# A last block of at most 64 keys with both parts of its weights on the partitions: layer 1's attention output in two passes instead of three

## The chip, the cores and the metric

The kernel runs on one core of one Trainium2 chip. The metric is the device time of one execution in microseconds. Before the change three runs took 1855.35, 1860.09 and 1863.01 us; their median, 1860.09 us, is the time before.

## What is computed

Two layers act on x (2 x 1024 x 512). Each adds an attention and a feed-forward part, both of the normalised x, to x. The change is in layer 1's attention, which has 32 heads of 128, in groups of four that share one of 8 key/value heads:

```python
scores = jnp.einsum('bhqd,bhkd->bhqk', q, k) * scale
scores = jnp.where(causal, scores, -1e9)
attn = jax.nn.softmax(scores, axis=-1)
out = jnp.einsum('bhqk,bhkd->bhqd', attn, v)
...
return out @ Wo.T
```

Inputs and outputs are float32. Layer 0 does a single-head attention without a mask beside a mixing of four streams with Sinkhorn normalisation; layer 1's feed-forward part is a dense product with routed low-rank terms.

## The kernel before

**Numbers in two parts.** Every float32 operand of a product is split into a float16 high part and a float16 low part, the rest. A product takes three matmuls (`PASSES`, line 81: high with high, high with low, low with high), added up in PSUM. `mm3` (line 88) issues them for all products but the attention output, which has its own loop, `attn_out` (line 345).

**Rows of layer 1.** `layer1_attn` walks 16 groups (2 batches x 8 key/value heads), each in 32 steps. A step s is one "row": 32 queries of each of the four heads, 128 partitions in all, against the first W = 32(s+1) keys, as the causal mask allows. Four steps make a block of 128 queries: c = s // 4 is the block, r = s % 4 the row in it. Rows r = 0 and 1 form half k = 0, rows 2 and 3 half k = 1. So the number of keys in the last block of 128 is 32, 64, 96 and 128 for r = 0 to 3; half k = 0 never has more than 64 of them. Constants named below: P = 128, S = 1024, LB = 3 buffers of `Phl`, XB = 4 of `xr`.

**One row.** `row_step` issues the scores of a row (tile `s` in PSUM), then the second part of the row before:

1. DVE (L283, L287) scales, masks and takes the row minimum into `P`; ACT takes the exponential and its sum (L291).
2. `rows_hi`: DVE takes the reciprocal (L302), ACT scales it (L303) and writes the weights' high part into `Phl` (L308).
3. `rows_lo`: DVE writes the low part into `Phl` in one instruction (L314); in layer 0 some rows use POOL (L312). If W is no multiple of 128, POOL fills the rest of both parts with zeros (L319), queued behind a DVE instruction. Then SP issues one DMA transpose (L320) of the row's 2m blocks of 128, m = ceil(W/128), high blocks first, low blocks after, into `PT`: keys on the partitions, queries along the row.

**Output.** `group_av` sums, for one half of block c, V's transposed blocks times `PT` into 256 columns of the PSUM tile `av`: c+1 blocks of keys, three matmuls each, 128 rows deep. After half 1, ACT and DVE turn `av` into two float16 parts `ao` (L104, L105) for the product with Wo (L88, result added to `acc` at L737).

**What sets the order.** `layer1_attn` writes out the order of work by hand: `at(g, s, f)` puts a piece of filling work after row step s of group g. Half k of block c's output stands at step 4c + 2k + 5, its product with Wo at 4c + 10; the next group's keys and values, its queries, and its weights stand in between; so do, in the first eight groups, layer 0's remaining mixing of batch 1, the gating and the feed-forward part (`put`, `extra`). V of a group (tile `V`, [128, part, block, 128]) is written during the group before. The Tile framework turns this into an order for each engine and allots buffers: a tile of a tag waits until one of the tag's buffers is free. The tag `xr` is used by the loads of batch 1's mixing (L607), for the gating's hidden values (L1063) and by eight normalised tiles for the gating in the seventh group (L1008).

**Queues.** SP issues all transposes and the loads of x; POOL issues the loads of weights; each engine works through its own instructions in order.

**The only matmuls with fewer rows.** Layer 0's output adds its bias with matmuls one row deep, `row` (1 x 128) times `bo` (1 x 512), at L484; the three matmuls of the product with Wo follow at L486.

Of the kernel before, what the change touches and what calls it, by code (L numbers as in the profile page):

```python
# [9 lines left out]
F16 = mybir.dt.float16  # L10
F32 = mybir.dt.float32
AF = mybir.ActivationFunctionType
ALU = mybir.AluOpType
# [3 lines left out]
P = 128  # L17
S = 1024
NB = 2
NT = S // P  # L20
# [8 lines left out]
FB, PB, LB, XB, WB = 4, 3, 3, 4, 9  # L29
QR = 32  # L30
# [21 lines left out]
def tile_model(ctx: ExitStack, tc: tile.TileContext, out: bass.AP, a: dict):  # L52


    nc = tc.nc
    V, A, G = nc.vector, nc.scalar, nc.gpsimd
# [7 lines left out]
    def T(tag, shape, dt=F32, bufs=None):  # L64
        count[0] += 1
        kw = {} if bufs is None else {"bufs": bufs}
        return sb.tile(shape, dt, tag=tag, name=f"{tag}_{count[0]}", **kw)
# [13 lines left out]
    PASSES = ((0, 0), (0, 1), (1, 0))  # L81
# [21 lines left out]
    def evac(src, hl_hi, hl_lo, scale):  # L103
        A.activation(hl_hi, src, AF.Copy, scale=scale)  # L104
        return V.scalar_tensor_tensor(hl_lo, src, scale, hl_hi, ALU.mult, ALU.subtract)  # L105
# [77 lines left out]
    last_hi, last_lo, last_low = [None], [None], [None]  # L183
# [8 lines left out]
    def behind(i, j, wait=False):  # L192

        kind = mybir.DependencyClass.Sync if wait else mybir.DependencyClass.NoSync
        tc.add_manual_dep(i.ins, j.ins.name, mybir.DependencyInfo(
            kind, mybir.DependencyReason.DATA), reason="behind")
# [69 lines left out]
    def share(got, n, k, make):  # L266

        if k % n == 0:
            got[0] = make()
        return got[0][:, k % n]  # L270

    P_of, hl_of = [None], [None]
# [21 lines left out]

    def rows_parts(W, n, k):

        m = -(-W // P)
        hl = share(hl_of, n, k, lambda: T("Phl", [P, n, 2 * S // n], F16, bufs=LB))
        return hl[:, :2 * m * P].rearrange("p (l k) -> p l k", l=2)

    def rows_hi(Pm, r, W, pool, hl):
        V.reciprocal(r[:, 1:2], r[:, 0:1])  # L302
        A.activation(r[:, 1:2], r[:, 1:2], AF.Copy, scale=PSCALE)  # L303
        if pool:
            A.activation(Pm[:, :W], Pm[:, :W], AF.Copy, scale=r[:, 1:2])
            A.activation(hl[:, 0, :W], Pm[:, :W], AF.Copy)
        else:
            A.activation(hl[:, 0, :W], Pm[:, :W], AF.Copy, scale=r[:, 1:2])  # L308

    def rows_lo(Pm, r, W, pool, hl, dst):  # L310
        if pool:
            G.tensor_tensor(hl[:, 1, :W], Pm[:, :W], hl[:, 0, :W], ALU.subtract)  # L312
        else:
            lo = V.scalar_tensor_tensor(hl[:, 1, :W], Pm[:, :W], r[:, 1:2], hl[:, 0, :W],  # L314
                                        ALU.mult, ALU.subtract)
            last_low[0] = lo
        if W < hl.shape[2]:

            behind(G.memset(hl[:, :, W:], 0.0), lo)  # L319
        nc.sync.dma_start_transpose(dst, hl.rearrange("p l k -> p (l k)"))  # L320

    pending = []

# [14 lines left out]
        count[0] += 1  # L338
        return ps.tile([P, 512], F32, tag="av", name=f"av_{count[0]}", bufs=BV)

    def attn_out(p, Vh, PT, nj):

        for j in range(nj):
            for k, (l, r) in enumerate(PASSES):
                nc.tensor.matmul(p, Vh(j, l), PT(r * nj + j),  # L345
                                 start=(j == 0 and k == 0),
                                 stop=(j == nj - 1 and k == 2))


    SC0 = 1.0 / (math.sqrt(128.0) * 1024.0)  # L350
# [331 lines left out]
    def fetch(src):  # L682
        st = T("f2k", [P, 512], bufs=FB)
        nc.gpsimd.dma_start(st, src)
        return st
# [42 lines left out]
    def qproj(b, w, Q, hh, half):  # L728

        p = proj_T(lambda c, l: w[:, l, c, :], xT1[b], half)  # L730
        evac(p.rearrange("p (b q) -> p b q", q=QR), Q[:, 0, :, hh, :], Q[:, 1, :, hh, :], 0.125)
# [6 lines left out]
        if last:  # L738
            nc.scalar.dma_start(out[(b * NT + t) * P:(b * NT + t + 1) * P, :], acc[b, t])

    def group_av(Vh, PT, c, k, p):


        attn_out(p.rearrange("p (h b q) -> p b h q", h=4, q=QR)[:, 2 * k:2 * k + 2].rearrange(
                     "p b h q -> p h b q"), lambda j, l: Vh[:, l, j, :],
                 lambda n: PT[:, n].rearrange("p b (h q) -> p h b q", q=QR), c + 1)
        if k == 0:
            return None
        ao = T("ao", [P, 2, 4, P], F16, bufs=2)
        hi, lo = [ao[:, l].rearrange("p h q -> p (h q)") for l in range(2)]  # L750
        evac(p, hi, lo, 1.0 / PSCALE)
        return ao
# [3 lines left out]
    def fetch_q(g, hh):  # L756
        qw[g, hh] = fetch(a["Wq"][4 * (g % NG) + hh])
# [8 lines left out]
    def layer1_attn(kv0, start, extra):  # L766


        N, NS = NB * NG, S // QR
        fill = {}  # L770

        def at(g, s, f):
            g, s = g + s // NS, s % NS
            fill.setdefault((g, s), []).append(f)

        kvs, Qs, PTs, avs, aos, wos = [{} for _ in range(6)]

        def q_unit(g, u):
            half, hh = divmod(u, 4)
            if hh == 0:  # L780
                Qs[g, half] = T("Q", [P, 2, NS // 2, 4, QR], F16, bufs=2)
            qproj(g // NG, qw[g, hh], Qs[g, half], hh, half)

        def fetch_wo(g, hh):
            n = 4 * (g % NG) + hh
            wos[g, hh] = fetch(a["WoT"][n * P:(n + 1) * P, :])

        def split_wo(g, hh):
            wos[g, hh] = parts_of(wos[g, hh], "wo", 32.0, WB)

        def av(g, c, k):
            if k == 0:
                avs[g, c] = out_tile()
            aos[g, c] = group_av(kvs[g]["V"], PTs[g, 2 * c + k], c, k, avs[g, c])

        def wo(g, c):
            wo_block(g // NG, c, aos[g, c], [wos[g, h] for h in range(4)], g % NG == NG - 1)

        kvs[0], fs = kv0
        start(fs[2:], lambda u: q_unit(0, u))  # L800
        for hh in range(4):
            fetch_wo(0, hh)
            split_wo(0, hh)
        for g in range(N):
            if g + 1 < N:
                new = (g + 1) % NG == 0
                kvs[g + 1], fs = kv((g + 1) // NG, (g + 1) % NG)
                at(g, KVN - 2 if new else 1, fs[0])
                for k, f in enumerate(fs[1:]):
                    at(g, KVN + 2 * k if new else 1 + 4 * k + 2 * (k == 0), f)  # L810
                for hh in range(4):
                    at(g, 5 + 4 * hh, lambda g=g, hh=hh: fetch_q(g + 1, hh))
                    at(g, 7 + 4 * hh, lambda g=g, hh=hh: split_q(g + 1, hh))
                for u in range(4):
                    at(g, QNN + 2 * u if new else QN + 4 * u, lambda g=g, u=u: q_unit(g + 1, u))
                for hh in range(4):
                    s = 26 + 2 * hh if new else 22 + 3 * hh
                    at(g, s - 2, lambda g=g, hh=hh: fetch_wo(g + 1, hh))
                    at(g, s, lambda g=g, hh=hh: split_wo(g + 1, hh))
            for u in range(4):  # L820
                at(g, QH + (1 if (g + 1) % NG == 0 else 3) * u, lambda g=g, u=u: q_unit(g, 4 + u))
            for c in range(NT):
                for k in range(2):
                    at(g, 4 * c + 2 * k + AVD, lambda g=g, c=c, k=k: av(g, c, k))
                at(g, 4 * c + WOD, lambda g=g, c=c: wo(g, c))
        for k, fs in extra.items():
            fill[k] = fs + fill.get(k, [])
        for g in range(N + 1):
            for s in range(NS):
                if g < N:  # L830
                    c, r = divmod(s, NR)

                    n = 4 if c < 2 else 2 if c < 4 else 1
                    if c < 4 and r == 0:
                        PT = T("PT", [P, 2 * (c + 1), NR, P], F16, bufs=3)
                        for k in range(2):
                            PTs[g, 2 * c + k] = PT[:, :, 2 * k:2 * k + 2]
                    elif c >= 4 and r % 2 == 0:
                        PTs[g, s // 2] = T("PT", [P, 2 * (c + 1), 2, P], F16, bufs=3)
                    Qt, q0 = Qs[g, s // (NS // 2)], s % (NS // 2)  # L840
                    row_step(lambda l: Qt[:, l, q0].rearrange("p h q -> p (h q)"),
                             kvs[g]["K"], QR * (s + 1), True, SC1, PTs[g, s // 2][:, :, r % 2], False, n, r)
                elif pending:
                    row_step()
                for f in fill.pop((g, s), []):
                    f()
        assert not fill, sorted(fill)
# [131 lines left out]
    PTs = attn0_rows(0, 0, *f0[0][:2], lambda: adv(CA))  # L979
    ys0 = branch0(0, *f0[0][3:5], lambda: adv(CB))  # L980
    attn0_out(0, 0, f0[0][2], PTs)
    PTs = attn0_rows(0, 1, *f0[0][:2], lambda: adv(CA))
# [6 lines left out]
    for half in range(2):  # L989
# [5 lines left out]
        PTs = attn0_rows(1, half, *f0[1][:2], lambda: adv(CD))  # L995
# [153 lines left out]
```

## Time and profile before

| what | value |
|---|---|
| median of the runs | 1860.09 us |
| the profiled execution | 1855.46 us |
| its span, first to last instruction | 1853.7 us |
| mean granted TensorE clock | 0.976 of full |
| TensorE busy | 1715.7 us |
| VectorE (DVE) busy | 1447.6 us |
| ScalarE (ACT) busy | 1194.1 us |
| GpSimd (POOL) busy | 910.6 us |
| DMA transposes `PT<-Phl` | 528, of them 512 in layer 1 |
| matmuls of the attention output (L345) | 3648, of them 3456 in layer 1 |

The profile is of one execution. PE is TensorE's matmuls, PEld its weight loads, which can run beside a matmul. A group of instructions is given as line, engine, operation, out<-in by the program's names, shapes, count, then busy time and the mean length of one in ns, then the engine's idle time just before them with what ended it. Matmuls overlap, so the mean length of one is longer than the distance between two. In a timeline a row is a run of like instructions: its start, its length, and in brackets the idle time before it. "issue" stands for time in which an engine waited for nothing that the profile shows.

### The profile page before, as it was taken

The page shows a single profiled execution, that of the slowest core. Times are in us where ns is not written, and L with a number is a line of the kernel's source. Part 1 is how long each engine was busy: PE and PEld are TensorE (multiplying, and loading weights), DVE is VectorE, ACT ScalarE, POOL GpSimd, SP SyncE. Part 2 cuts the span into 40 slices and gives each one's busy share as a digit, 9 for nine tenths or more (in the row PEclk, how much of TensorE's full clock was granted, in tenths as well). Part 3 has the DMA queues.
Part 4 walks back from the last instruction along what each step waited for, and adds up shares of the span by engine and source line. Part 5 has one row for each costly group of instructions (what it writes and reads, how often), then busy time and mean ns, then how long its engine had stood idle before and what let it go on. Part 6 is the DMA issues. An engine that isn't in the chain of part 4 may idle for free. (4 is left out here: it accounts for less than half of the span.)

```text
span 1853.7 us, 35094 instructions
## 1 busy us (share of the span) xinstructions
PE 1715.7 (93%) x11458; PEld 1046.0 (56%) x11458; DVE 1447.6 (78%) x4050; ACT 1194.1 (64%) x2917; POOL 910.6 (49%) x1540
## 2 busy tenths in 40 slices
PE   4756399999999999998999999999999999999998
PEld 3434146566666556655555556666666666656565
DVE  8888978988888877777976867777777777777675
ACT  3848665656676778776544756666666767676554
POOL 5567639768775455647634333424242433335200
PEclk9878699999999999999999999999999999999999
DMA  7435225666574657468546555656565656566455
GB/s 211 82 56 124 67 51 131 143 115 144 113 147 102 143 115 158 111 131 158 137 92 141 130 120 126 146 111 150 107 151 115 142 117 140 117 141 139 101 123 120
DMA packets 707306, 230.26 MB, mean 124 GB/s; under 512 B 689953, under 2 KB 690081, under 8 KB 707122
## 3 DMA queue, kind: packets, MB, share of 16 engines
q1 hardware_dynamic: 691666, 180.75, 47.2%
q0 software_dynamic: 13152, 43.07, 8.5%
q10 hardware_dynamic: 2304, 4.20, 0.7%
q8 instruction: 90, 1.47, 0.4%
q14 instruction: 94, 0.77, 0.1%
HBM read 52.81 MB, written 4.19 MB: 31 GB/s over the span
## 5 line engine op out<-in xcount | busy, mean ns | idle before, releaser
L291 ACT ACTIVATE P<-P,nm 128x1024 f32<-128x1024 f32 (+31 forms) x528 | 391.3, 742 | 250.0 <-DVE nm L283 234.8
L314 DVE SCALAR_TENSOR_TENSOR Phl<-P,r,Phl 128x1024 f16<-128x1024 f32 (+31 forms) x515 | 434.4, 853 | 85.9 <-ACT Phl L308 79.5
L88 PE MATMUL s<-K,Q 128*128 128x512 f16 (+22 forms) x2400 | 440.7, 317 | 19.5 <-DVE P L287 11.6
L345 PE MATMUL av<-PT,V 128*128 128x256 f16 x3648 | 447.7, 274 | 7.5 <-DMA PT<-Phl 6.8
L345 PEld LDWEIGHTS <-V 128*128 128x128 f16 x3648 | 357.0, 98 | 94.7 <-DMA PT<-Phl 8.3
L308 ACT ACTIVATE Phl<-P,r 128x1024 f16<-128x1024 f32 (+31 forms) x515 | 370.0, 731 | 22.3 <-DMA PT<-Phl 3.3
L88 PE MATMUL pp<-xT,wq 128*128 128x512 f16 x1536 | 372.9, 381 | 6.3 <-DVE acc L737 3.2
L88 PE MATMUL pp<-wo,ao 128*128 128x512 f16 x1536 | 369.9, 379 | 2.9 <-ACT ao L104 2.7
L94 POOL TENSOR_SCALAR f2k<-f2k 128x512 f32<-128x512 f32 x164 | 109.5, 668 | 499.9 <-DVE Phl L314 444.5
L88 PEld LDWEIGHTS <-Q 128*128 128x128 f16 x2400 | 223.2, 98 | 178.2 <-issue 28.4
L88 PEld LDWEIGHTS <-wq 128*128 128x128 f16 x1536 | 149.6, 98 | 173.8 <-issue 8.5
L88 PEld LDWEIGHTS <-ao 128*128 128x128 f16 x1536 | 149.4, 98 | 156.5 <-ACT ao L104 4.8
L287 DVE TENSOR_SCALAR_CACHE_REDUCE P<-s 128x512 f32<-128x512 f32 (+15 forms) x272 | 152.6, 562 | 21.7 <-PE s L88 19.7
L283 DVE CUSTOM_DVE_ANT_0 P<-s,mask,nm 128x272 f32<-128x272 f32 (+15 forms) x256 | 157.3, 615 | 8.7 <-PE s L88 1.0
L303 ACT ACTIVATE r<-r 128x1 f32<-128x1 f32 x528 | 96.2, 193 | 66.2 <-DVE r L302 65.4
L319 POOL MEMSET Phl<- 128x192 f16 (+2 forms) x384 | 72.6, 209 | 133.5 <-DMA PT<-Phl 95.7
L302 DVE RECIPROCAL r<-r 128x1 f32<-128x1 f32 x528 | 79.2, 155 | 75.3 <-ACT P L291 72.1
L104 ACT ACTIVATE ao<-av 128x512 f16<-128x512 f32 x128 | 75.1, 587 | 92.2 <-PE av L345 92.0
L283 DVE CUSTOM_DVE_ANT_0 P<-s,mask 128x32 f32<-128x32 f32 (+15 forms) x256 | 104.3, 432 | 27.6 <-PE s L88 27.1
L104 ACT ACTIVATE Q<-pp 128x512 f16<-128x512 f32 x128 | 74.5, 582 | 76.7 <-PE pp L88 72.2
L737 DVE SCALAR_TENSOR_TENSOR acc<-pp,acc 128x512 f32<-128x512 f32 x128 | 87.4, 682 | 41.0 <-PE pp L88 40.6
L105 DVE SCALAR_TENSOR_TENSOR Q<-pp,Q 128x512 f16<-128x512 f32 x128 | 87.6, 684 | 34.9 <-ACT Q L104 34.6
(254 smaller groups left out, 2119.1 us busy)
## 6 DMA issues: line engine op xcount, KB each, us to landing
f2k<-in_Wq POOLq DMA_DIRECT2D x64, 256.0 KB, 3.2
f2k<-in_WoT POOLq DMA_DIRECT2D x64, 256.0 KB, 3.3
PT<-Phl SPq DMA_TRANSPOSE x528, 3.2
acc<-in_x SPq DMA_DIRECT2D x16, 256.0 KB, 4.6
f2k<-in_Wup POOLq DMA_DIRECT2D x16, 256.0 KB, 3.5
out<-acc ACTq DMA_DIRECT2D x16, 256.0 KB, 3.5
xr<-in_x SPq DMA_DIRECT2D x12, 256.0 KB, 4.1
f2k<-in_Wlat POOLq DMA_DIRECT2D x8, 256.0 KB, 5.5
```

The lines of the kernel that those rows point to most:

```text
L88: nc.tensor.matmul(dst, lhs(l), rhs(r), start=(i == 0 and j == 0), stop=(i == n - 1 and j == 2))
L94: first = G.tensor_scalar(stage, stage, scale, 1.0, ALU.mult, ALU.mult)
L104: A.activation(hl_hi, src, AF.Copy, scale=scale)
L105: return V.scalar_tensor_tensor(hl_lo, src, scale, hl_hi, ALU.mult, ALU.subtract)
L283: last_row[0] = V.tensor_tensor_reduce(Pm[:, o:o + w], pt[:, :w], mask[:, 512 - w:], -scale, first, ALU.add, ALU.min, nm[:, k:k + 1])
L287: last_row[0] = V.tensor_scalar(Pm[:, o:o + w], pt[:, :w], -scale, first, ALU.mult, ALU.min, accum_out=nm[:, k:k + 1])
L291: A.activation(Pm[:, :W], Pm[:, :W], AF.Exp, bias=last, scale=-1.0, accum_out=r[:, 0:1])
L303: A.activation(r[:, 1:2], r[:, 1:2], AF.Copy, scale=PSCALE)
L308: A.activation(hl[:, 0, :W], Pm[:, :W], AF.Copy, scale=r[:, 1:2])
L314: lo = V.scalar_tensor_tensor(hl[:, 1, :W], Pm[:, :W], r[:, 1:2], hl[:, 0, :W], ALU.mult, ALU.subtract)
L345: nc.tensor.matmul(p, Vh(j, l), PT(r * nj + j), start=(j == 0 and k == 0), stop=(j == nj - 1 and k == 2))
L737: V.scalar_tensor_tensor(acc[b, t], p, 1.0 / 256.0, acc[b, t], ALU.mult, ALU.add)
```

## The change

For rows with 1 to 64 keys in the last block (32 and 64, so half k = 0), that block of `Phl` is laid out anew: its first 64 columns hold the high part, the other 64 the low part of the same keys. The row then has 2c+1 blocks: c high ones, the mixed one, c low ones. The transpose puts the mixed block's two parts on partitions 0 to 63 and 64 to 127.

The output's last block then takes two matmuls: V's high part, standing twice on the partitions, times the whole mixed block (128 rows), and V's low part times the high weights (partitions 0 to 63, 64 rows). The doubled V is a tile `Vm` of tag `xr`, filled once in a group by two SBUF-to-SBUF copies of 64 partitions on SP's queue, placed at step 2. DVE writes the low part of such a row in two pieces where c > 0. The zero fill covers what is left of each 64: two times 32 columns for W % 128 = 32, nothing for 64. Rows with 96 or 128 keys in the last block, and all of layer 0, stay as they are.

```diff
     def rows_parts(W, n, k):
+        c, w = divmod(W, P)
+        hl = share(hl_of, n, k, lambda: T("Phl", [P, n, 2 * S // n], F16, bufs=LB))
+        if 0 < w <= 64:
+            hl = hl[:, :(2 * c + 1) * P]
+            o = c * P
+            lo = [(o, W, hl[:, o + 64:o + 64 + w])]
+            if c:
+                lo.insert(0, (0, o, hl[:, o + P:]))
+            pad = hl[:, o:o + P].rearrange("p (l k) -> p l k", l=2)[:, :, w:] if w < 64 else None
+            return hl, hl[:, :W], lo, pad
         m = -(-W // P)
-        hl = share(hl_of, n, k, lambda: T("Phl", [P, n, 2 * S // n], F16, bufs=LB))
-        return hl[:, :2 * m * P].rearrange("p (l k) -> p l k", l=2)
+        hl = hl[:, :2 * m * P]
+        v = hl.rearrange("p (l k) -> p l k", l=2)
+        return hl, v[:, 0, :W], [(0, W, v[:, 1, :W])], v[:, :, W:] if W < m * P else None
...
     def rows_lo(Pm, r, W, pool, hl, dst):
-        if pool:
-            G.tensor_tensor(hl[:, 1, :W], Pm[:, :W], hl[:, 0, :W], ALU.subtract)
-        else:
-            lo = V.scalar_tensor_tensor(hl[:, 1, :W], Pm[:, :W], r[:, 1:2], hl[:, 0, :W],
-                                        ALU.mult, ALU.subtract)
-            last_low[0] = lo
-        if W < hl.shape[2]:
-
-            behind(G.memset(hl[:, :, W:], 0.0), lo)
-        nc.sync.dma_start_transpose(dst, hl.rearrange("p l k -> p (l k)"))
+        whole, hi, los, pad = hl
+        for a0, a1, lo in los:
+            if pool:
+                G.tensor_tensor(lo, Pm[:, a0:a1], hi[:, a0:a1], ALU.subtract)
+            else:
+                last_low[0] = V.scalar_tensor_tensor(lo, Pm[:, a0:a1], r[:, 1:2], hi[:, a0:a1],
+                                                     ALU.mult, ALU.subtract)
+        if pad is not None:
+
+            behind(G.memset(pad, 0.0), last_low[0])
+        nc.sync.dma_start_transpose(dst[:, :whole.shape[1] // P], whole)
...
-    def attn_out(p, Vh, PT, nj):
-
-        for j in range(nj):
-            for k, (l, r) in enumerate(PASSES):
-                nc.tensor.matmul(p, Vh(j, l), PT(r * nj + j),
-                                 start=(j == 0 and k == 0),
-                                 stop=(j == nj - 1 and k == 2))
+    def attn_out(p, Vh, PT, nj, mixed=None):
+        full = nj - (mixed is not None)
+        todo = [(Vh(j, l), PT(r * nj + j)) for j in range(full) for l, r in PASSES]
+        if mixed is not None:
+            todo += [(mixed, PT(full)), (Vh(full, 1)[:64], PT(full)[:64])]
+        for k, (v, pt) in enumerate(todo):
+            nc.tensor.matmul(p, v, pt, start=(k == 0), stop=(k == len(todo) - 1))
...
-                 lambda n: PT[:, n].rearrange("p b (h q) -> p h b q", q=QR), c + 1)
+                 lambda n: PT[:, n].rearrange("p b (h q) -> p h b q", q=QR), c + 1,
+                 None if k else Vm[:, c])
...
+        def twice(g):
+            Vm = kvs[g]["Vm"] = T("xr", [P, NT, P], F16, bufs=XB)
+            for k in range(2):
+                nc.sync.dma_start(Vm[64 * k:64 * k + 64], kvs[g]["V"][0:64, 0])
...
+            at(g, 2, lambda g=g: twice(g))
```

## The prediction

> **What bounds the kernel now.** I read the page's busy times first, then busy time in two stretches of layer 1, then the instruction groups by shape, then the chain of waits inside one group, then the timeline around the only matmuls with few rows.
>
> The page's part 1, each engine's busy time:
>
> ```profile
> PE 1715.7 (93%) x11458; PEld 1046.0 (56%) x11458; DVE 1447.6 (78%) x4050; ACT 1194.1 (64%) x2917; POOL 910.6 (49%) x1540
> ```
>
> A busy TensorE need not be a full one, so I look at stages. Layer 1's rows begin at 262 us (first score matmul of 32 columns) and its sixteen groups take some 92 us each; the later groups start at 1086. Busy time in two stretches (columns: PE, PEld, DVE, ACT, POOL, granted clock, DMA share, GB/s):
>
> ```profile
> 262.00:1086.00 824.00, 796.30 (x5384) 485.75 (x5382) 667.60 (x1837) 544.49 (x1376) 499.09 (x889) 0.99 0.59 129
> 1086.00:1800.00 714.00, 713.79 (x4768) 442.21 (x4766) 528.76 (x1460) 467.09 (x1139) 250.82 (x460) 1.00 0.59 127
> ```
>
> In the second stretch TensorE never rests; in the first it rests 27.7 us of 824 and DVE is 81% busy. Whether it runs at its own pace shows in the chain of one group (1178 to 1270), which is TensorE alone:
>
> ```profile
> 1182.20 2.62 PE av L345 x24
> 1184.82 4.53 PE pp L88 x21
> ```
>
> 2.62/24 is 0.109 us for a matmul of 256 columns, 4.53/21 is 0.216 us for one of 512: time follows the columns. So TensorE sets layer 1's time, and every matmul added or taken away counts nearly in full.
>
> **The change: passes taken away.** The attention-output group:
>
> ```profile
> L345 PE MATMUL av<-PT,V 128*128 128x256 f16 x3648 | 447.7, 274 | 7.5 <-DMA PT<-Phl 6.8 <-DVE ao L105 0.6
> ```
>
> 3456 of the 3648 are layer 1's (16 groups x 2 halves x 3 x 36 blocks). The half k=0 (rows 0 and 1 of each four, 32 and 64 keys in the last block) takes two passes for that block instead of three: one matmul less in each of 16 x 8 = 128 sums. The chain's pace values them at 128 x 0.109 = -14.0 us; the group's busy share (447.7/3648 = 0.123) would give -15.7, but holds the ends of runs. I take -14.0. Their weight loads are hidden.
>
> **The change: a matmul of 64 rows.** Of the two passes left, one reads 128 rows (both weight parts against V doubled), the other only 64. Every other layer-1 matmul has 128 rows. No 64-row matmul stands in the trace; the nearest row is layer 0's bias (L484), one row deep among 128-row matmuls. TensorE timeline at 91 us, then the weight loads there (start, length, in brackets the idle time before):
>
> ```profile
> 91.09 0.71 PE L345 MATMUL av<-PT,V 128*128 128x256 f16 x5
> 91.73 0.60 PE L484 MATMUL pp<-wo,row 1*128 1x512 f16 x2
> 92.27 0.82 PE L486 MATMUL pp<-wo,wo 128*128 128x512 f16 x3
> 93.02 1.03 PE L484 MATMUL pp<-wo,row 1*128 1x512 f16 x4
> ```
>
> ```profile
> 91.09 0.42 PEld L345 LDWEIGHTS <-V 128*128 128x128 f16 x4
> 91.73 0.11 PEld L484 LDWEIGHTS <-row 1*128 1x128 f16 x2 [0.21 <-issue]
> 92.26 0.33 PEld L486 LDWEIGHTS <-wo 128*128 128x128 f16 x3 [0.42 <-issue]
> 93.02 0.33 PEld L484 LDWEIGHTS <-row 1*128 1x128 f16 x3 [0.42 <-issue]
> ```
>
> Five av matmuls from 91.09 should free the array at 91.09 + 5 x 0.109 = 91.635; the one-row matmul starts at 91.73, 0.095 late. Two of 512 columns from there end at 92.162; the 128-row one starts at 92.27, 0.108 late. Three more end at 92.918; the next one-row matmul starts at 93.02, 0.102 late. Inside a run of equal rows nothing is lost. The second view shows how: within a run the next weights load while a matmul runs, at a change of row count they load only after it, with an idle gap put down to no releaser. A change costs about 0.10 us, in either direction.
>
> The 64-row matmul comes last in its sum: 128 rows before it, 128 rows after it, so two changes each, 128 x 2 x 0.10 = +25.6 us. Bounds: 0 if 64 rows need no change of the array, 0.11 if each costs the worst seen (+28.2); below nothing is excluded, as the matmul streams the same 256 columns.
>
> Two rules of the Trainium skill bear on this. "TensorE: Matmul & The Clock Gate", section "Why this matters for your kernels", says a single matmul of 32 rows takes as long as one of 128: by that alone the sum stays -14.0. "TensorEngine Tiling (Array Packing)", section "Key Properties", speaks against the change: going to another tiling mode drains the engine, and its "Tiling Modes" gives 64 rows a mode of their own. It states no price; if I estimate a drain as the 128 cycles that the first page gives for the array's depth, at its 2.4 GHz, that is 0.053 us, 128 x 2 x 0.053 = +13.7, and the sum is about nothing. The row has 0.10 for the same kind of change, so I take +25.6, net **+11.7 us** on TensorE.
>
> **The change: VectorE.** The low part of a half-0 row falls into two pieces where full blocks precede it (c >= 1): 7 x 2 more instructions in a group, 224 in all. The timeline around 1180 us has this instruction at two widths:
>
> ```profile
> 1181.37 1.29 DVE L314 SCALAR_TENSOR_TENSOR Phl<-P,r,Phl 128x1024 f16<-128x1024 f32 x1
> ...
> 1183.70 0.24 DVE L314 SCALAR_TENSOR_TENSOR Phl<-P,r,Phl 128x32 f16<-128x32 f32 x1
> ```
>
> (1.29 - 0.24)/992 = 1.06 ns for an element, so 0.21 us whatever the width, and 224 x 0.21 = 47 us more on DVE, 2.9 in each group. In the groups from 1086 on DVE is 74% busy and covers it: nothing. In the first eight groups it is 23.5 us on an engine with 156 us idle; it waits in line only where TensorE already stalls on DVE. Bounds 0 and 23.5; the waits view for TensorE there puts some 22 of 824 us down to DVE, 2.7%, which is 0.6 us, and I take +1.
>
> **The change: POOL, transposes, copies.** The zero fill of the 64-wide rows goes, that of the 32-wide ones shrinks to 64 elements:
>
> ```profile
> L319 POOL MEMSET Phl<- 128x192 f16 x128 | 33.6, 263 | 65.5 <-DMA PT<-Phl 41.3 <-DVE nm L283 19.3 <-DVE Phl L314 4.9
> L319 POOL MEMSET Phl<- 128x128 f16 x128 | 26.8, 209 | 22.2 <-DMA PT<-Phl 13.8 <-DVE P L287 8.3
> ```
>
> 128 x 0.209 + 128 x (0.263 - 0.156) = 40 us off POOL, which is 35% busy after 1086 and waits for others most of the time. Likewise 256 of the 512 layer-1 transposes lose one block of 2c+2. Neither is in the chain: 0 (a gain of a microsecond or so where a transpose was last).
>
> New are two SBUF copies of V in each group, 32 in all, on SP's queue between the transposes. Nearest rows:
>
> ```profile
> PT<-Phl SPq DMA_TRANSPOSE x528, 3.2
> ...
> xr<-in_x SPq DMA_DIRECT2D x12, 256.0 KB, 4.1
> ```
>
> The xr loads hold SP 0.58 us each (median in the tile view), so the transposes queued behind two copies come about 1.2 us later, and the copies (128 KB each) land some 4 us after issue. The first mixed matmul waits for them, and behind it in TensorE's order stand the next scores and projections. V itself is written about 48 us before the group. From the issue of a group's second transpose to the group's first av matmul I count 10 to 13 us in most groups, but 4.3 in the first and 3.2 in the eighth: covered in fourteen, 0 to 2 us in those two. The copy also holds one of four xr buffers all through its group; in the seventh group (824 to 946) the gating's tiles want four themselves, so some of these tiles come later, in a group where TensorE is already idle 14.5 us: 0 to 6. I take +1 for all this; if the cover of the copies were gone everywhere it would be 16 x 4 = 64 us.
>
> **The sum.** -14.0 + 25.6 + 1 + 1 = +13.6 us. The profiled execution took 1855.46 us (1853.7 of span and 1.8 around it); +13.6 makes 1869.1, a ratio of 1.0073. That execution is at the low end of the runs shown (1855.35 to 1863.01); on their median, 1860.09, the ratio gives **1874 us**.
>
> **Rivals.**
> 1. *No price for 64 rows.* One mechanism: the array treats 64 rows as it treats 128, with the weights loaded under the matmul before. Place: the last matmul of the 128 half-0 sums. It decides at a change below 0.055 us (two of them equal the 0.109 saved). Then -14.0 + 2 = -12, 1848 us: faster. For it: the only rows seen are for one row, not 64, and 64 could be handled otherwise. Against: the gap comes with a change of the row count, in both directions. Chance 0.17.
> 2. *Half price*, about 0.055 each, as the drain estimate: -14 + 14 + 2 = +2, 1862 us, no change to see. Chance 0.13.
> 3. *VectorE becomes the bound* of the first eight groups, its 23.5 us in full beside the array's 11.7: +37, 1897 us. For it: most of TensorE's named waits there (22 of 29 us) are on DVE. Against: DVE has 156 us idle. Chance 0.04.
>
> My forecast, a full price: 0.66, with a range of its own of 1866 to 1883 us. That fewer matmuls run is not in doubt: the loops fix the count.
>
> **Chances.** The range 1850 to 1883 leaves out about two thirds of rival 1, rival 3 and the ends of my own case: some 0.19. A measurement of this kernel can tell about 0.5% (9.3 us) from no change. Slower by more: most of case 0 and rival 3, 0.60. Faster by more: most of rival 1, 0.15. Within: rival 2 and the edges, 0.25.
>
> **What would show it.** av matmuls at 3520, 128 of them as 64*128; the timeline around one should have 0.20 us more than 2 x 0.109 from the start of the matmul before it to the start of the one after it, and the weight loads at both sides an idle gap with "issue". The chain of a late group should stay all TensorE, its period growing from 91.8 us by 8 x 0.09 = 0.7. DVE's busy time should rise by 47 us, POOL's fall by 40. I am wrong if weight loads of 64 rows run under the matmul before (period shorter by 0.9), or if the first eight groups grow by more than 1.5 us each (DVE, or the copies).

## The result, and the profile after

The changed kernel took 1879.54 us (median of 4 runs, 1878.23 to 1880.73) against 1861.55 us before: 1.0100 of the time before, interval 1.0077 to 1.0123. It is slower, by 18 us (about 1%); forecast were 1874 us and 1.0073. The profiled execution took 1878.23 us, 22.8 more than the one of before, which lay at the low end of its runs.

Part 1 of the page, busy time of each engine:

```profile
PE 1731.1 (92%) x11330; PEld 1022.7 (55%) x11330; DVE 1503.9 (80%) x4274; ACT 1193.9 (64%) x2917; POOL 876.8 (47%) x1412
```

TensorE has 128 matmuls fewer and is busy 15 us longer. DVE has its 224 instructions more. The output's matmuls by shape (busy time, mean ns, idle before):

```profile
L363 PE MATMUL av<-PT,V 128*128 128x256 f16 x3264 | 403.5, 274 | 9.5 <-DMA PT<-Phl 8.1 <-DVE ao L105 1.3
L363 PE MATMUL av<-PT,V 64*128 64x256 f16 x128 | 35.9, 280 | 0.0
L363 PE MATMUL av<-PT,xr 128*128 128x256 f16 x128 | 34.9, 273 | 0.0
```

35.9/128 is 0.280 us of busy time for a 64-row matmul, against 403.5/3264 = 0.124 for one of 128 rows in the first row: the 64-row ones hardly overlap their neighbours. Where that comes from shows in the timelines of TensorE and of its weight loads around one of them (start, length, idle time before in brackets):

```profile
1139.25 0.82 PE L363 MATMUL av<-PT,V 128*128 128x256 f16 x6
1139.90 0.27 PE L363 MATMUL av<-PT,xr 128*128 128x256 f16 x1
1140.11 0.28 PE L363 MATMUL av<-PT,V 64*128 64x256 f16 x1
1140.32 1.04 PE L88 MATMUL pp<-wo,ao 128*128 128x512 f16 x4
```

```profile
1139.80 0.10 PEld L363 LDWEIGHTS <-xr 128*128 128x128 f16 x1
1140.11 0.09 PEld L363 LDWEIGHTS <-V 64*128 64x128 f16 x1 [0.21 <-issue]
1140.32 0.76 PEld L88 LDWEIGHTS <-ao 128*128 128x128 f16 x5
```

The six ahead start 0.109 apart. From the mixed matmul to the 64-row one it is 0.21, and 0.21 again to the next: two matmuls' time for each. The weights of the 64-row matmul, and the first of those after it, start together with their matmul and not under the one before. Over all 128 of them the two steps are 0.205 and 0.212 us in the median, 0.096 and 0.103 more than the 0.109 us of 256 columns; 25.5 us in sum.

The stages that answer to the two of before (busy time of PE, PEld, DVE, ACT, POOL; granted clock; DMA):

```profile
261.00:1103.00 842.00, 806.16 (x5328) 475.06 (x5328) 699.08 (x1951) 547.32 (x1378) 480.61 (x825) 0.99 0.59 124
1103.00:1817.00 714.00, 714.00 (x4658) 426.99 (x4656) 549.07 (x1552) 460.01 (x1131) 236.03 (x398) 1.00 0.58 124
```

The first eight groups take 841.4 us instead of 824.2 (from the first score matmul of the first group to that of the ninth), 17.2 more. From there to the end it is 773.7 instead of 767.6, 6.1 more, with TensorE as full as it was. So three quarters of the loss between the two profiled executions lie where TensorE was not full. (The one of before lies 6 us below its median. The late groups repeat closely from run to run, so of the 18 us between the medians some 12 are left for the stage ahead of them, as an estimate.) Most of that is the seventh and eighth group, where the rest of layer 0 and the gating are filled in. Before, then after:

```profile
823.90:946.00 122.10, 107.57 (x783) 67.24 (x781) 102.56 (x276) 72.50 (x175) 82.47 (x116) 0.96 0.70 146
946.00:1086.10 140.10, 137.34 (x862) 78.30 (x863) 97.20 (x250) 75.43 (x183) 48.01 (x77) 1.00 0.54 119
```

```profile
826.10:964.50 138.40, 119.07 (x824) 71.98 (x823) 109.18 (x299) 72.65 (x175) 76.81 (x106) 0.91 0.66 128
964.50:1102.70 138.20, 132.45 (x809) 72.22 (x807) 101.10 (x261) 76.40 (x183) 47.14 (x70) 1.00 0.55 118
```

262.2 us became 276.6. In the seventh group TensorE is idle 19.3 us instead of 14.5, and its granted clock falls from 0.96 to 0.91: 0.09 x 138.4 - 0.04 x 122.1 = 7.6 us of clock time lost on top. Work also moved between the two groups: the seventh holds 41 matmuls more and the eighth 53 fewer, so they are best read together. The named wait that grew most in the seventh is the one of the weight loads for the transposes of the gating's tiles (total, times, longest; before, then after):

```profile
PEld L88 <- DMA wo<-xr: 2.8, 1, 2.8
```

```profile
PEld L88 <- DMA wo<-xr: 7.6, 3, 5.2
```

### The profile page after: what moved, and what is told of

Same layout as the page of the kernel before. It is cut to its first block, busy times and chain, and to the rows that moved or that the text cites. A ratio compares the mean times of both kernels' runs of the same rounds, so it can differ in the third digit from the quotient of the medians.

```text
span 1876.4 us, 35001 instructions
## 1 busy us (share of the span) xinstructions
PE 1731.1 (92%) x11330; PEld 1022.7 (55%) x11330; DVE 1503.9 (80%) x4274; ACT 1193.9 (64%) x2917; POOL 876.8 (47%) x1412
## 4 chain that ended last, share of the span: by engine, by line
PE 48%; DVE 4%; ACT 3%; issue 2%; POOL 2%; DMA 2%; POOLq 0%; ACTq 0%; DVEq 0%
PE pp L88 26%; PE av L363 12%; PE s L88 11%; DVE Phl L329 2%; ACT Phl L321 1%; ACT P L291 1%; ACT f2k L649 1%; DMA wo<-xr 1%; DVE P L283 1%; DVE P L287 1%; DMA PT<-Phl 1%; DMA f2k<-in_Wq 0%; DVE cmp L105 0%; POOL f2k L94 0%; POOL xr L240 0%
## 5 line engine op out<-in xcount | busy, mean ns | idle before, releaser
L329 DVE SCALAR_TENSOR_TENSOR Phl<-P,r,Phl 128x64 f16<-128x64 f32 (+9 forms) x739 | 491.1, 698 | 71.7 <-ACT Phl L321 65.1
L363 PE MATMUL av<-PT,V 128*128 128x256 f16 (+1 forms) x3392 | 439.2, 275 | 9.5 <-DMA PT<-Phl 8.1
L363 PEld LDWEIGHTS <-V 128*128 128x128 f16 (+1 forms) x3392 | 330.8, 98 | 119.0 <-issue 35.3
L94 POOL TENSOR_SCALAR f2k<-f2k 128x512 f32<-128x512 f32 x164 | 113.4, 692 | 541.3 <-DVE Phl L329 514.9
L88 PEld LDWEIGHTS <-ao 128*128 128x128 f16 x1536 | 143.6, 98 | 170.5 <-ACT ao L104 6.9
L283 DVE CUSTOM_DVE_ANT_0 P<-s,mask 128x32 f32<-128x32 f32 (+15 forms) x256 | 103.8, 430 | 17.0 <-PE s L88 16.9
L88 PEld LDWEIGHTS <-xT 128*128 128x128 f16 x864 | 63.7, 103 | 76.1 <-DMA xT<-wo 44.0
```

What stands on the lines that cost most here:

```text
L88: nc.tensor.matmul(dst, lhs(l), rhs(r), start=(i == 0 and j == 0), stop=(i == n - 1 and j == 2))
L94: first = G.tensor_scalar(stage, stage, scale, 1.0, ALU.mult, ALU.mult)
L283: last_row[0] = V.tensor_tensor_reduce(Pm[:, o:o + w], pt[:, :w], mask[:, 512 - w:], -scale, first, ALU.add, ALU.min, nm[:, k:k + 1])
L329: last_low[0] = V.scalar_tensor_tensor(lo, Pm[:, a0:a1], r[:, 1:2], hi[:, a0:a1], ALU.mult, ALU.subtract)
L363: nc.tensor.matmul(p, v, pt, start=(k == 0), stop=(k == len(todo) - 1))
```

## The experiments

All times are medians, each with the kernel before on the same chip (1857.6 to 1859.3 us). "Seventh and eighth group" is the stretch just shown, "late period" the mean time of the tenth to fifteenth group, both from each run's trace. The stages are read from one execution of each kernel; work that was left unchanged differed there by some 3 us in the first eight groups (the last run below), so smaller differences in that stage say little.

**The tiles read earlier.** The changed kernel with

```diff
-                put(0, s + t + GL, lambda t=t: gating_h(hs[1], t, gw1, dts[t]))
+                put(0, s + t + 2, lambda t=t: gating_h(hs[1], t, gw1, dts[t]))
```

> The changed kernel, but each of the eight gating tiles of the seventh group is read two steps after it is made, not three, so that two xr buffers are enough for them beside the doubled V and the hidden values. Theory 1 (the doubled V takes the fourth xr buffer, and the tiles wait for it): the seventh group falls from 138 us back to some 123, and the kernel to about 15 us below the changed one, near 1864 us (1.002 of before). Theory 2 (the seventh group grows by DVE's extra pieces): it stays near 138 us and the kernel near 1.010 of before. Theory 3 (the tiles' transposes are late whatever the buffers are, and now are read sooner): longer than 138.

Measured: 1879.32 us, 1.0095 (1.0078 to 1.0112). The seventh group fell from 138.4 to 130.8 us and the eighth grew from 138.2 to 142.5; together they are 3.4 us shorter. The weight loads now wait 2.1 us for the gating's tiles, less than before the change, and the loss is still there: less demand on the xr buffers moves it into the next group and hardly reduces it. Theory 1 falls as the main cause. Theory 2 has the time right, but not the seventh group by itself.

**128 rows.** The changed kernel with

```diff
-            todo += [(mixed, PT(full)), (Vh(full, 1)[:64], PT(full)[:64])]
+            todo += [(mixed, PT(full)), (Vh(full, 1), PT(full))]
```

> The changed kernel with its last pass 128 rows deep (V's low part of all 128 keys times the whole mixed block; it adds products of two low parts, of the order of the rounding). As many matmuls, no change of row count in layer 1. If the change of row count costs 0.096 + 0.103 us as the changed kernel's trace has it: 128 x 0.199 = 25.5 us off the changed kernel, to about 1854 us, 0.996 of before; the late groups' period from 92.6 to 90.9 us. If the 64-row matmul only fills time that TensorE would lose anyway: no change from 1.010.

Measured: 1861.99 us, 1.0011 (0.9998 to 1.0023), and a late period of 90.9 us instead of 92.6 in the changed kernel and 91.8 before. The late period fell by the 1.7 expected (8 x 0.199 = 1.6). The whole fell by about 17 us, not 25.5: in the profiled executions 13.1 us from the ninth group on, 6.0 in the first eight, where there is idle time. The seventh and eighth group stayed long:

```profile
824.40:962.20 137.80, 118.01 (x826) 73.34 (x824) 108.53 (x300) 72.36 (x175) 77.14 (x107) 0.91 0.64 130
962.20:1098.20 136.00, 130.94 (x807) 72.90 (x805) 100.47 (x261) 76.10 (x183) 46.05 (x70) 1.00 0.54 120
```

They take 273.8 us (262.2 before); the six ahead of them take 561.6, as before the change (562.0). So this version gains 7.0 us from the ninth group on and loses 11.6 in the seventh and eighth, and the kernel gains nothing to see.

**Both.** The two edits together, the one of the tiles and the one of the 128 rows.

> The changed kernel with both: 128-row last pass and the tiles read after two steps. If the two causes add up: 25.5 + 15 us below the changed kernel, about 1839 us, 0.988 of before. If the seventh group is held by something else: as the 128-row run alone, 0.996.

Measured: 1862.07 us, 1.0008 (0.9994 to 1.0022). The second line of the expectation came, nothing beside the 128-row pass (which itself stands at 1.001, not at 0.996).

**64 rows alone.** The kernel before with

```diff
-                nc.tensor.matmul(p, Vh(j, l), PT(r * nj + j),
+                m = 64 if short and j == nj - 1 and k == 2 else P
+                nc.tensor.matmul(p, Vh(j, l)[:m], PT(r * nj + j)[:m],
```

(`short` is k == 0 of `group_av`).

> The kernel before with one edit: in the half with at most 64 keys in its last block, the third pass of that block reads 64 rows instead of 128 (the other rows are zeros). As many matmuls, nothing else moved. Theory 1 (each change of row count costs 0.10 us): 128 x 0.199 = +25.5 us, 1.0137 of before. Rival (64 rows are free by themselves and the cost came with the new order or the copies): 1.000.

Measured: 1.0099 (1.0075 to 1.0124), 1880.86 us; the changes of row count cost 0.096 and 0.103 us again, and the late period is 93.47, 1.67 over before. That is less than the 1.0137 expected: from the ninth group on the profiled execution lost 13.1 us, but in the first eight groups 4, not 12.7. That execution (1874.47 us) was 6 us faster than the median, so the usual loss there may be larger than 4.

**Three passes of 64 rows.** The same edit for all three passes of that block.

```diff
-                m = 64 if short and j == nj - 1 and k == 2 else P
+                m = 64 if short and j == nj - 1 else P
```

> The kernel before, with all three passes of that last block 64 rows deep: 384 matmuls of 64 rows instead of 128 in the run with one, but again one change to 64 and one back for each sum. If the change costs: as the run with one, about 1.011 of before, the late groups' period 93.5 us. If each 64-row matmul costs: three times that run's loss, 1.03, the period near 96.8 us.

Measured: 1875.26 us, 1.0072 (1.0055 to 1.0089), below the 1.011 expected, but far from 1.03; the late period 93.47, the same to the hundredth. The weight loads of the run with one and of the run with three:

```profile
L346 PEld LDWEIGHTS <-V 64*128 64x128 f16 x128 | 11.8, 92 | 27.5 <-issue 27.5
```

```profile
L346 PEld LDWEIGHTS <-V 64*128 64x128 f16 x384 | 26.2, 94 | 33.5 <-issue 29.5 <-DVE r L302 1.2 <-DVE nm L283 0.4
```

Three times as many 64-row matmuls, and the idle time put to "issue" stays: it is the change that costs, not the 64 rows.

**Copies alone.** The kernel before with the doubled V in its xr buffer (`twice`, as in the change), read by two passes of the last block:

```diff
+                v = twin if twin is not None and j == nj - 1 and k < 2 else Vh(j, l)
-                nc.tensor.matmul(p, Vh(j, l), PT(r * nj + j),
+                nc.tensor.matmul(p, v, PT(r * nj + j),
```

> The kernel before with only the doubled V added: the two copies in each group into an xr buffer, read by the first two passes of the last block in the half with at most 64 keys there (the weights are zero beyond 64 rows, so the sums stay the same). Rows, transposes, DVE's pieces and the 128-row passes stay. Before, the seventh and eighth group take 262 us together, 277 in the changed kernel. Theory 1 (the xr buffers hold up the gating tiles): about 274 us together, 1.006 of before. Theory 2 (DVE's extra pieces): 262 us, 1.000.

Measured: 1865.92 us, 1.0036 (1.0023 to 1.0049). The seventh and eighth group take 263.5 us, 1.3 more than before: the buffers hold up the gating tiles little. The second group takes 103.8 instead of 98.5, though DVE is no busier there (84%, 86% before). TensorE waits there once, for 6.3 us, for a transpose (`PT<-Phl`), a wait that the second group of before does not have. So the copies cost something, mostly elsewhere than I had looked for it; why that transpose comes late is not shown.

**Two pieces alone.** The kernel before with

```diff
-            lo = V.scalar_tensor_tensor(hl[:, 1, :W], Pm[:, :W], r[:, 1:2], hl[:, 0, :W],
-                                        ALU.mult, ALU.subtract)
+            o = W // P * P if 0 < W % P <= 64 else 0
+            for a0, a1 in [(0, o), (o, W)] if o else [(0, W)]:
+                lo = V.scalar_tensor_tensor(hl[:, 1, a0:a1], Pm[:, a0:a1], r[:, 1:2], hl[:, 0, a0:a1],
+                                            ALU.mult, ALU.subtract)
```

> The kernel before with only DVE's low part of a row with 1 to 64 keys in the last block written in two pieces (224 instructions of 0.21 us fixed length more). Theory 2 (DVE's extra pieces lengthen the seventh and eighth group): 274 us instead of 262 together, 1.006 of before. Theory 1: 262 us together, 1.000 to 1.001, and the groups from the ninth on at 91.8 us either way.

Measured: 1878.59 us, 1.0099 (1.0080 to 1.0117), more than was expected of it, with no other part of the change. Its seventh, eighth, and ninth to fourteenth groups:

```profile
834.70:966.80 132.10, 114.90 (x803) 71.43 (x802) 111.79 (x299) 72.89 (x175) 78.74 (x116) 0.92 0.69 139
966.80:1109.30 142.50, 135.84 (x843) 76.05 (x842) 103.63 (x262) 76.11 (x183) 49.09 (x77) 1.00 0.54 116
1109.30:1660.30 551.00, 551.00 (x3675) 342.17 (x3674) 436.46 (x1212) 367.06 (x889) 196.84 (x358) 1.00 0.59 130
```

In the last row DVE has 24 us more than the same six groups before (412.86) and TensorE stays full, 91.8 us a group: nothing is lost. In the seventh and eighth group DVE has 15.7 us and 38 instructions more; 28 of these are the pieces, the others are work that falls into a longer stretch. The two groups take 12.4 us more, and the clock in the seventh stands at 0.92. The six groups ahead of them take 572.0 us instead of 562.0.

**Two pieces, not in the seventh group.** The same with the two pieces left out where g is 6.

```diff
-            o = W // P * P if 0 < W % P <= 64 else 0
+            o = W // P * P if 0 < W % P <= 64 and not plain[0] else 0
...
+                    plain[0] = g == 6
```

> The kernel before with DVE's low part in two pieces, as in the run with that alone (1.0099 of before), except in the seventh group. If the loss sits in that group's gating work on DVE: the seventh and eighth group take 262 us instead of 275, the kernel about 1.003 of before. If the pieces of all the first eight groups count alike (18 us over eight groups): about 1.008.

Measured: 1873.15 us, 1.0073 (1.0058 to 1.0089). The seventh and eighth group fell to 266.6 us from 274.6; the six ahead of them stayed at 571.1. So of the 22 us that the pieces cost in the first eight groups of the profiled execution, 8 come with the 14 pieces of the seventh group, more than their eighth part, and 9 stay in the first six. Both expectations were too simple: the loss neither sits in the seventh group alone nor is spread evenly.

**The small piece on POOL.** The 128-row run with

```diff
+            elif a0:
+                G.tensor_scalar(Pm[:, a0:a1], Pm[:, a0:a1], r[:, 1:2], 1.0, ALU.mult, ALU.mult)
+                G.tensor_tensor(lo, Pm[:, a0:a1], hi[:, a0:a1], ALU.subtract)
```

> The changed kernel with the last pass 128 rows deep (it adds products of two low parts, of the order of the rounding) and the small second piece of the low part (32 or 64 columns) made by POOL in two instructions instead of by DVE. DVE's busy time goes back by about 50 us, POOL's grows by some 60 to 110. Theory 2 (DVE's time in the crowded groups): the seventh and eighth group fall from 274 us in the 128-row run to some 262, the kernel from 1.001 to about 0.994 of before. Rival (the pieces hurt because the low part is done later, whichever engine does it, or because of the order that comes with them): 274 us and 1.001 stay, or worse where POOL is queued.

Measured: 1869.64 us, 1.0060 (1.0043 to 1.0078), slower than with the piece on DVE (1.0011). Part 1 of its page:

```profile
PE 1711.3 (92%) x11330; PEld 1034.8 (55%) x11330; DVE 1448.3 (78%) x4050; ACT 1192.6 (64%) x2917; POOL 1058.8 (57%) x1860
```

DVE is back at its time before (1447.6), but POOL has 185 us more than in the 128-row run (874.0). The first eight groups take 840.5 us against 835.4 with the piece on DVE: the seventh and eighth are shorter (269.6 against 273.8), the six ahead of them longer (570.9 against 561.6). The run doesn't tell DVE's time from the low part's being finished later: it took away DVE's time, but put the pieces behind POOL's other work.

**The seventh group in the old way.** The 128-row run, with neither new layout nor doubled V where g is 6.

```diff
-        if 0 < w <= 64:
+        if 0 < w <= 64 and not plain[0]:
...
-                 None if k else Vm[:, c])
+                 None if k or Vm is None else Vm[:, c])
...
+            if g != 6:
+                at(g, 2, lambda g=g: twice(g))
...
+                    plain[0] = g == 6
```

> The changed kernel with the last pass 128 rows deep (it adds products of two low parts, of the order of the rounding), and the seventh group done in the old way: three passes, no doubled V, no extra pieces. If the loss of the seventh and eighth group comes from that group's own doubled V or pieces: 262 us together, 1848 us, 0.994 of before. If the neighbours' copies, which are issued into the seventh group too, hold it up: near 270 us, about 0.999.

Measured: 1854.13 us, 0.9969 (0.9954 to 0.9983). Its seventh and eighth group:

```profile
824.00:946.10 122.10, 107.61 (x795) 67.22 (x794) 104.84 (x284) 72.38 (x175) 78.67 (x115) 0.99 0.68 150
946.10:1088.20 142.10, 136.28 (x843) 76.78 (x842) 98.83 (x262) 75.37 (x183) 45.98 (x70) 0.98 0.55 114
```

The seventh group is back at 122.1 us, the two take 264.2 together, near the 262 of the first expectation. The other groups keep the new layout, the six ahead at 561.1 us. This version is faster than both kernels. The run leaves out the seventh group's pieces, copies and short sum together, so it doesn't say which of them lengthens it; the runs with one part alone point to the pieces.

**New layout in the late groups only.** The same, with the old way in all of the first eight groups.

```diff
-            if g != 6:
+            if g >= 8:
...
-                    plain[0] = g == 6
+                    plain[0] = g < 8
```

> The new layout with the 128-row last pass (it adds products of two low parts, of the order of the rounding) only in the eight groups from the ninth on, the old way in the first eight. Theory (the saved matmul counts where TensorE alone sets the time, and DVE's pieces cost where DVE is crowded): the first eight groups as before, 824 us from the first score to the ninth group, the last ones at 90.9 instead of 91.8 us each: 7 us less, 0.996 of before. Rival (the saving in the first eight groups pays for the pieces there): slower than the run that keeps only the seventh group in the old way, 0.997 or more.

Measured: 1849.80 us, 0.9959 (0.9944 to 0.9974). In two stretches, busy time as above:

```profile
264.00:1092.00 828.00, 798.57 (x5391) 486.30 (x5391) 669.21 (x1838) 545.30 (x1377) 498.64 (x888) 0.99 0.60 128
1092.00:1852.00 760.00, 754.37 (x5009) 464.79 (x5005) 586.22 (x1646) 488.49 (x1182) 235.14 (x403) 1.00 0.58 125
```

From the ninth group to the end 760.7 us instead of 767.6: the 7 us expected. The first eight groups, unchanged in their work, took 827.4 (824.2 before; executions of one kernel differ by that much). This is the version with the lowest median; its interval overlaps that of the run before it, so which of the two is better is not settled.

## Why the prediction was right, and where not

Right: the direction, and the time inside the range. The mechanism on TensorE was right too. But one of the prediction's own signs of being wrong came true: the first eight groups grew by 17.2 us, 2.1 each, over the 1.5 that it allowed. That the total came near is in part luck. By its steps:

- **Passes taken away**, -14.0 us, 0.109 each. The count came (3520). Where TensorE is the bound it is exact: 8 x 0.109 = 0.87 us a group, and the 128-row runs have 90.92 against 91.80. What it brings in the first eight groups can't be read off, since no run has it alone.
- **The matmul of 64 rows**, +25.6 us. Measured 0.096 + 0.103 for each, 25.5 in sum. The one-row matmuls of layer 0 were the right row; the estimate of half that from the Trainium skill's figures ("TensorEngine Tiling (Array Packing)", "Key Properties", with the array's depth of "TensorE: Matmul & The Clock Gate") was too small, though its rule that a change of mode drains the engine fits what is seen: no weights are loaded under the matmul before a change. Whether the time lost is the drain or the weight load that no longer hides (0.09 to 0.10 us in the timeline) the traces don't tell. What failed is that I took all of it for the path. It counts in full from the ninth group on (13.1 us between the changed kernel and the 128-row run, where 64 x 0.199 = 12.7 is the full cost), and by about half before (6.0), where TensorE has idle time.
- **TensorE's net, +11.7.** For the late half I had 5.8; measured 6.1.
- **VectorE, +1 us: this step failed.** The pieces are longer than I gave: 47 us forecast, 56 more busy, 0.25 us each and not 0.21. In the late groups they cost nothing, as said. In the first eight groups I weighed them by the 2.7% of time that TensorE is seen waiting for DVE. That is the wrong measure: alone, the pieces cost 0.99%, some 18 us, nearly all of it in the first eight groups (22.4 us between the profiled executions), where +1 was forecast. The two ends that I kept were 0 and 23.5, and the truth is near the upper one. A likely reason, not shown by a run, is that the rows, the gating and the mixing hang on one another through DVE there, so that more DVE time makes new waits. The falling TensorE clock goes with it (0.96 to 0.92 in the seventh group).
- **Copies and buffers, +1 us.** Alone 0.36%, 6 to 7 us. Landing in 2.4 us instead of the 4 assumed, they were not late for the mixed matmul (no idle time before it in the changed kernel's row above). With them alone, the seventh group was 2.8 us longer, within what unchanged work differs by, and the second 5.3.
- **POOL and transposes, 0.** POOL's zero fills took 38.2 us instead of 80.4, the forecast 40 less. No run tests this part alone.

The parts taken alone add up to 0.99 + 0.99 + 0.36 % less the saved 0.75 (the forecast 14.0 of 1860, not measured as a whole), 1.6%, and the change as a whole is 1.00% (0.77 to 1.23). They overlap; that in the first eight groups each fills idle time that another has made would explain it, but is argued and not shown. So my sum came near because one term was too small and another too large: +1 for DVE, and +25.6 for TensorE counted everywhere.

Rival 1, no price for 64 rows, fell with the timeline: that short matmuls take no longer than full ones holds in these runs only between matmuls of the same row count. Rival 2, half price, fell for the array but describes what reaches the end in the first eight groups. Rival 3, DVE as the bound there at +23.5 us, was given 0.04; the pieces alone took 22.4 us in the first eight groups, so its cost was there, and only the overlap with the other parts kept the whole at 17.2. Open stays whether DVE's time or the later end of the low part does it, and why the copies lengthen the second group.

## What to carry to other kernels

On a TensorE that is never idle, a matmul with another row count costs about 0.2 us here, since neither its own weights nor those of the next matmul load in hiding, and that outweighs a saved matmul of 256 columns (0.109 us). Fill the rows up instead, or put matmuls of that row count next to each other: three in a row cost as much as one. A small fixed cost on a second engine must be priced in the stage where that engine is crowded; here it came out near its full length, and the share of waits in the profile of before was no measure of it. And a change may be right for one stage and wrong for another: with the last pass 128 rows deep, it gains 0.4% where it is kept to the late groups and 0.3% where the seventh group alone is left out.

## What the runs showed of the hardware

A change of row count between TensorE matmuls cost 0.096 us going from 128 to 64 rows and 0.103 us coming back, and the next weights were not loaded under the matmul before. A second and a third 64-row matmul in a row cost nothing more: three of them and one had the same period of 93.47 us a group.

A longer idle time on TensorE can be charged twice. In the seventh group the windows of half clock in the traces' clock record sum to 10 us before and to 24 us after. Of the 16 us that the group grew by, 5 are idle time, about 7 are matmuls at half pace, and the rest is work that moved into it. The sum of idle time alone doesn't set the clock, though: with the seventh group in the old way TensorE was idle for 14.5 us as before, and the half-clock windows there summed to 3 us.
